# Attention scores accumulated in one bank per head from key differences, with row sums in bursts

## The chip, the cores and the metric

One core of a Trainium2 chip runs the whole kernel. The metric is device time in microseconds, the median over runs; the profile comes from one further execution. The engines are TensorE (PE, with its weight loads PEld), VectorE (DVE), ScalarE (ACT), GpSimd (POOL) and SyncE (SP), whose queue issues most of the DMAs.

## The reference, cut to what matters

A transformer block with conditioning: x is [2, 2048, 512], 16 heads of 32 dimensions, causal attention, then an MLP with hidden width 2048.

```python
mod = silu(condition) @ Wada + bada          # six vectors per batch row
xm  = layernorm(x) * (1 + sc_a) + sh_a
q, k, v = split_heads(xm @ Wqkv)
scores  = where(causal, q @ k.T * hd**-0.5, -inf)
x = x + gt_a * (concat(softmax(scores) @ v) @ Wproj + bproj)
x = x + gt_m * (gelu(modulated_layernorm(x) @ W1 + b1) @ W2 + b2)
```

Everything is float32. The change concerns the scores, the softmax's row sums, and how keys are written and loaded.

## The kernel before, in words

**Stages.** For each of the two batch rows: the QKV products (class `Qkv`), then the attention (`attention_phase`), then the projection. The MLP for both rows comes last. While one row's QKV runs, the first scores of that row are already made.

**QKV.** Four groups (`g`) of 512 tokens. For each group and each chunk `f` of four heads, the q and the k product (four accumulating matmuls each, into a bank named ps_qk) are split into a high and a low part, both in float32r (`hl`, lines 820 to 826: ACT writes the high part, DVE the rest), and written to DRAM by one DMA. Keys and queries are later loaded back so that the 128 partitions hold the 32 dimensions of a head four times, in the combinations high/low of q with high/low of k. One float32r matmul over 128 partitions then gives the score at full precision. `load_keys` does this for keys (`kst`), `load_queries` for queries (`qst`). Two key buffers take turns by chunk.

**Units.** A unit is one chunk of four heads with one block `i` of 512 queries: 16 units per batch row. The softmax needs the row maxima, so each score is computed twice:

- With queries on the partitions (tile `s`, `Row.bank`, `Row.score`): a matmul into a score bank (pool `ps_s`, two banks), then DVE takes the maximum over the keys (`mx`, line 461; with the causal mask on the diagonal block, line 456). These are made up to three units ahead (`AHEAD`). `due` and `count` decide how many are put into each step of the attention, by a cost in about DVE nanoseconds. `Row.rows` turns a unit's maxima into a row vector `fold` (high and low part by head and query tile).
- With keys on the partitions (tile `st`, `scores_t`): for each step, that is each tile `j` of 128 keys, and each of the four heads, a first matmul of 32 partitions (`sel` and `fold`) writes minus the maximum into the head's bank, and a second one adds the score of the keys `kst` with the queries `qst`. ACT then writes the exponential `e` (line 586). On the diagonal, where a key tile meets fewer queries, the tiles that start at query 128 and at 384 share a step and a bank; GpSimd zeroes what lies above the diagonal (line 592).

**After the exponentials.** Two steps later (`LAG`) the values product `o` (`values`, matmuls of 32 columns, one per head, in plain float32) and the row sums `sm` (a product with ones, `row_sums`) follow. For the sums, the exponentials of four full key tiles are first added up (`ee`, line 614, on GpSimd; on DVE in a row's last unit), so that one sums product serves four tiles. `sm` accumulates in a bank of its own through the whole unit; `finish` copies `o` and `sm` out and stores them.

**Order.** Matmuls and most of the work in the attention keep the order in which the program writes them (`keep_in_program_order`, by `mm` and `act`). In a step that is: four folds, then st matmuls and scores alternating, then what `flush` finds due (values and sums), then the remaining scores. Other instructions, those of QKV among them, are ordered by the tile framework. DMAs go into SP's queue in order.

**Banks of PSUM in the attention.** Two for scores, four for st, one for o, one for sm. A score may also borrow an st bank (`borrow`); in the last unit st also uses the score banks.

Of the kernel before, what the change touches and what calls it, by code (L numbers as in the profile page):

```python
# [17 lines left out]
P = 128  # L18
# [9 lines left out]
def dit_block_kernel(  # L28
# [49 lines left out]
    EE_BUFS = 8  # L78
# [5 lines left out]
    def pool(name, bufs=1, **kw):  # L84
# [21 lines left out]
    tmask = bp.tile([P, TQ + 1], F32, tag="tmask", name="tmask")  # L106
    nc.vector.tensor_reduce(
        tmask[:, :TQ],
# [4 lines left out]
    nc.vector.tensor_copy(tmask[:, TQ:], tmask[:, TQ - 1 : TQ])  # L113
    fold, mhl = [], []
    for n in range(2):

        f = bp.tile([P, QB + P], F32R, tag=f"fold{n}", name=f"fold{n}")
        fold.append(f)
# [9 lines left out]
    def picks():  # L128
# [36 lines left out]
        [dram.tile([2, P, T], F32, tag=f"k{b}{c}", name=f"k{b}{c}") for c in range(C)]  # L165
        for b in range(B)
# [38 lines left out]
    def act(ins):  # L205

        return tc.keep_in_program_order(ins)
# [22 lines left out]
    def transposed(pool_, psum, xts, n0, mv, rstd, a, c, b, dst, xns=None):  # L230
# [8 lines left out]
        for t, xt in enumerate(xts):  # L239
            if by_act:  # L240
                continue
            xn = pool_.tile([P, D], F32, tag="xn", name="xn", bufs=3)
            n = n0 + t
            nc.vector.tensor_scalar(
                xn, xt, mv[:, n, 0:1], rstd[:, n : n + 1], ALU.subtract, ALU.mult
            )
            xns.append(xn)
# [41 lines left out]
    class Row:  # L289


        def __init__(self, b):
            self.b = b
            self.vv = bp.tile([P, NT, D], F32, tag="vv", name="vv")
            self.kst, self.qst, self.pools = {}, {}, {0: bp}
# [8 lines left out]
            self.mx = None  # L304
            self.spent = 0
            self.rows_made = 0

        def load_keys(self, c, g, n=1):

            tok = slice(g * MT, (g + n) * MT)  # L310
            if g == 0:
                self.kst[c] = self.pools[c % 2].tile(
                    [P, HC, T], F32R, tag=f"kst{c % 2}", name="kst"
                )
            for r in range(4):
                nc.sync.dma_start(
                    self.kst[c][r * HD : (r + 1) * HD, :, tok].bitcast(F32),
                    kd[self.b][c][r % 2, :, tok].rearrange("(h d) t -> d h t", d=HD),
# [123 lines left out]
        def bank(self, u, h, t, kb, s):  # L442
# [6 lines left out]
                self.kst[c][:, h, kb * QB : kb * QB + w],  # L449
# [41 lines left out]
        def score(self, n, borrow=None):  # L491

            for k in range(n):
                if borrow and k % 2 == 0:
                    s = borrow()
                else:
                    s = ps_sp.tile([P, QB], F32, tag="s", name="s")  # L500
                item = self.todo.pop(0)
                u = item[0]
                if self.mx is None:
                    self.mx = bp.tile(
                        [P, HC * TQ, units[u][1] + 1], F32, tag="mx", name="mx", bufs=3
                    )
                self.bank(*item, s)
                if not self.todo or self.todo[0][0] != u:
# [4 lines left out]
        def rows(self, u):  # L513
# [8 lines left out]
                fold[u % 2].rearrange("p (t q) -> p t q", t=TQ + 1),  # L522
                ps.unsqueeze(1).to_broadcast([P, TQ + 1, P]),
                tmask.unsqueeze(2).to_broadcast([P, TQ + 1, P]),
# [11 lines left out]
    def attention_phase(row):  # L536
        b, vv, kst, qst = row.b, row.vv, row.kst, row.qst
        with pool(f"att{b}") as ap, pool(
            f"ps_st{b}", bufs=HC, space=PSUM
        ) as ps_stp, pool(f"ps_o{b}", space=PSUM) as ps_op:  # L540
            row.pools[1] = ap

            n_bank = [0]

            def scores_t(u, step, n):
# [6 lines left out]

                def st_bank():

                    n_bank[0] += u == len(units) - 1
                    if n_bank[0] % 6 >= HC:
                        return ps_sp.tile([P, QB], F32, tag="s", name="st")
                    return ps_stp.tile([P, QB], F32, tag="st", name="st")  # L560

                c, i = units[u]
                tiles = steps_of[u][step]
                q0 = tiles[0][1]
                w = sum(QB - q for _, q in tiles)
                sts, es = [], []
                for h in range(HC):
                    g = slice(h * HD, (h + 1) * HD)
                    st = st_bank()
                    mm(  # L570
                        st[:, :w], sel[g, :], fold[u % 2][g, q0 : q0 + w],
                        start=True, stop=False,
                    )
                    sts.append(st)
                for h in range(HC):
                    at = 0
                    for j, q in tiles:
                        mm(
                            sts[h][:, at : at + QB - q],
                            kst[c][:, h, j * P : (j + 1) * P],  # L580
                            qst[u][:, h, q:],
                            start=False, stop=at + QB - q == w,
                        )
                        at += QB - q
                    e = ap.tile([P, QB], F32, tag="e", name="e", bufs=E_BUFS)
                    act(nc.scalar.activation(e[:, :w], sts[h][:, :w], AF.Exp))  # L586
                    if tiles[0][0] >= i * TQ:

                        d = e.rearrange("p (t k) -> p t k", k=P)[:, 0 : TQ : TQ - 1, :]
                        d = d[:, : len(tiles), :]  # L590
                        act(
                            nc.gpsimd.affine_select(  # L592
                                d, d, pattern=[[0, len(tiles)], [1, P]],
                                compare_op=ALU.is_ge, fill=0.0,
                                base=0, channel_multiplier=-1,
                            )
                        )
                    es.append(e)
                    if h < 2 and n >= 3 or h >= HC - n and n < 3:
                        row.score(1)  # L600
                if n >= 3:
# [1137 lines left out]
```

## Time and profile before

| | |
|---|---|
| median of 3 runs | 2367.9 us (2367.5 to 2370.27) |
| profiled execution | 2366.88 us, span 2365.2 us |
| granted TensorE clock | 1.00 |
| TensorE busy | 2336.9 us (99%) |
| VectorE, ScalarE, GpSimd busy | 1397.6, 924.1, 1079.2 us |
| fold matmuls (512 and 256 wide) | 1024 and 128 |
| sums matmuls of added tiles | 192, seen as 384 |

The page shows busy time as a union: where matmuls overlap, the time is counted once. A plain float32 matmul is recorded as two matmuls, a float32r matmul as one. In the rows of groups the columns are the line, the engine, the operation, what it writes and reads, the shape and the count, then busy us and mean ns of one, then idle time of the engine before these instructions and what ended it. Line 203 is the helper through which all matmuls go, so groups are told apart by their tiles.

### The profile page before, as it was taken

How to read it: one execution, taken by the hardware profiler on the slowest of the kernel's cores; microseconds unless marked ns; L12 is line 12 of the kernel's file. 1: busy time of each engine (PE TensorE's matmuls, PEld its weight loads, DVE VectorE, ACT ScalarE, POOL GpSimd, SP SyncE). 2: the span in 40 equal slices, each digit the busy share in tenths (PEclk: the TensorE clock that was granted, in tenths of full speed). 3: DMA queues.
4: the chain of work that ended last, by engine and by line, in shares of the span. 5: the costliest groups of instructions: out<-in, count | busy, mean ns of one | idle time of the engine just before them, and what ended most of it. 6: DMA issues, size and time to landing. Idle time of an engine off the chain costs nothing.

```text
span 2365.2 us, 32348 instructions
## 1 busy us (share of the span) xinstructions
PE 2336.9 (99%) x11469; PEld 1294.6 (55%) x11469; DVE 1397.6 (59%) x2868; ACT 924.1 (39%) x1736; POOL 1079.2 (46%) x1219
## 2 busy tenths in 40 slices
PE   8999999999999999999999999999999999999998
PEld 4455555555544445555555555444585486487477
DVE  3466666767656636576666766553483374365356
ACT  2113555555555012155555555613322332332321
POOL 1052997978793646379887997460000000000000
PEclk9999999999999999999999999999999999999999
DMA  7577215151223788650513214272254254353433
GB/s 258 188 249 195 49 28 118 27 117 46 83 106 132 255 259 259 220 113 24 117 46 85 59 31 144 78 252 100 98 170 146 94 179 139 119 166 132 135 124 129
DMA packets 134106, 311.49 MB, mean 132 GB/s; under 512 B 14208, under 2 KB 29100, under 8 KB 129080
## 3 DMA queue, kind: packets, MB, share of 16 engines
q1 hardware_dynamic: 126096, 277.13, 38.9%
q0 software_dynamic: 7472, 31.75, 3.7%
q8 instruction: 90, 1.47, 0.3%
q14 instruction: 72, 0.59, 0.1%
q10 hardware_dynamic: 376, 0.55, 0.1%
HBM read 229.95 MB, written 87.29 MB: 134 GB/s over the span
## 4 chain that ended last, share of the span: by engine, by line
PE 96%; DVE 2%; POOL 1%; issue 0%; DMA 0%; ACT 0%; SPq 0%; POOLq 0%; ACTq 0%; DVEq 0%
PE st L203 20%; PE ps_a L203 17%; PE o L203 11%; PE s L203 10%; PE ps_qk L203 9%; PE ps_b L203 9%; PE ps_v L203 5%; PE ps_o L203 5%; PE ps_c L203 4%; PE sm L203 4%; PE ps_xt L211 1%; POOL ee L614 1%; PE ps_o L211 1%; DVE mx L461 0%; DVE junk L456 0%
## 5 line engine op out<-in xcount | busy, mean ns | idle before, releaser
L586 ACT ACTIVATE e<-st 128x512 f32<-128x512 f32 (+1 forms) x1152 | 574.6, 578 | 428.1 <-PE st L203 361.6
L614 POOL TENSOR_TENSOR ee<-ee,e 128x512 f32<-128x512 f32 x424 | 529.2, 1289 | 4.4 <-ACT e L586 4.0
L461 DVE TENSOR_REDUCE mx<-s 128x1 f32<-128x512 f32 x604 | 407.9, 688 | 204.5 <-PE s L203 203.1
L203 PE MATMUL s<-kst,qst 128*128 128x512 f32 (+3 forms) x1032 | 463.7, 451 | 5.7 <-DVE mx L461 2.9
L203 PE MATMUL st<-qst,kst 128*128 128x512 f32 (+3 forms) x1280 | 409.4, 387 | 0.0
L203 PE MATMUL ps_a<-sum,w 128*128 128x256 f32 (+1 forms) x1088 | 346.6, 454 | 0.0
L203 PE MATMUL o<-e,vv 128*32 128x512 f32 (+3 forms) x2560 | 300.5, 538 | 2.0 <-POOL e L592 2.0
L456 DVE CUSTOM_DVE_ANT_0 junk<-s,causal 128x512 bf16<-128x512 f32 (+3 forms) x428 | 209.3, 489 | 135.5 <-PE s L203 127.6
L203 PEld LDWEIGHTS s<-kst,qst 128*128 128x128 f32 x1032 | 194.4, 189 | 155.7 <-DVE mx L461 55.6
L203 PEld LDWEIGHTS st<-qst,kst 128*128 128x128 f32 x1280 | 227.3, 188 | 94.2 <-issue 62.2
L203 PEld LDWEIGHTS ps_a<-sum,w 128*128 128x128 f32 x1088 | 206.3, 190 | 109.8 <-issue 91.4
L614 POOL TENSOR_TENSOR ee<-e 128x512 f32<-128x512 f32 x168 | 210.4, 1285 | 101.4 <-ACT e L586 101.0
L203 PE MATMUL ps_qk<-xmT,wqkv 128*128 128x512 f32 x512 | 239.0, 594 | 1.8 <-DVE xmT L263 1.8
L592 POOL TENSOR_SCALAR_AFFINE_SELECT e<-e 128x128 f32<-128x128 f32 (+1 forms) x384 | 122.4, 357 | 135.0 <-ACT e L586 132.3
L203 PE MATMUL st<-fold,sel 32*128 32x512 f32 (+1 forms) x1152 | 149.1, 481 | 0.9 <-ACT vv L843 0.5
L203 PEld LDWEIGHTS ps_qk<-xmT,wqkv 128*128 128x128 f32 x512 | 93.9, 190 | 97.0 <-issue 90.4
L1318 DVE TENSOR_TENSOR h<-c,ps_b 128x512 f32<-128x512 f32 x32 | 22.0, 687 | 202.4 <-PE ps_b L203 202.4
L203 PEld LDWEIGHTS st<-fold,sel 32*128 32x128 f32 x1152 | 59.3, 181 | 144.8 <-ACT e L586 86.6
L203 PE MATMUL ps_v<-wqkv,xmT 128*128 128x512 f32 x256 | 122.3, 594 | 0.0
L203 PE MATMUL ps_b<-sum,w 128*128 128x256 f32 (+1 forms) x384 | 120.6, 450 | 0.0
L203 PEld LDWEIGHTS o<-e,vv 128*32 128x32 f32 x2560 | 61.1, 108 | 102.0 <-issue 81.0
L1492 ACT ACTIVATE h<-h,cols 128x512 f32<-128x512 f32 x96 | 69.2, 721 | 118.6 <-DVE h L1318 118.6
(155 smaller groups left out, 2601.3 us busy)
## 6 DMA issues: line engine op xcount, KB each, us to landing
qst<-q SPq DMA_DIRECT2D x128, 256.0 KB
w<-w1d SPq DMA_DIRECT2D x32, 896.0 KB
w<-w2d SPq DMA_DIRECT2D x28, 1024.0 KB
kst<-k SPq DMA_DIRECT2D x24, 1024.0 KB
w<-w2d SPq DMA_DIRECT2D x28, 768.0 KB
q<-hl SPq DMA_DIRECT2D x32, 512.0 KB
k<-hl SPq DMA_DIRECT2D x32, 512.0 KB
w2d<-w POOLq DMA_DIRECT2D x28, 448.0 KB, 6.5
```

The costliest lines, as they stand in the source:

```text
L203: return tc.keep_in_program_order(nc.tensor.matmul(*args, **kw))
L211: return tc.keep_in_program_order(nc.tensor.transpose(dst, src, ident[:n, :n]))
L456: nc.vector.tensor_tensor_reduce(junk[:, :w], s[:, :w], causal[:, QB - w :], 1.0, MASKED, ALU.add, ALU.max, m,)
L461: nc.vector.tensor_reduce(m, s[:, :w], axis=AX.X, op=ALU.max)
L586: act(nc.scalar.activation(e[:, :w], sts[h][:, :w], AF.Exp))
L592: nc.gpsimd.affine_select(d, d, pattern=[[0, len(tiles)], [1, P]], compare_op=ALU.is_ge, fill=0.0, base=0, channel_multiplier=-1,)
L614: act(engine.tensor_tensor(dst, x, y, ALU.add))
L1318: act(nc.vector.tensor_tensor(dst, x, y, ALU.add))
L1492: nc.scalar.activation(d, ps, AF.Gelu, bias=col(r_b1 + half * HF + f, 1))
```

## The change

1. **Key differences.** QKV also writes, for each chunk, `g`: the difference of the keys at token t and at token t - 128, split into high and low parts (`gaps`; `tails` carries the last 128 keys from group to group). It is loaded into one buffer `kgap` for the attention. The old buffer `kst` holds the plain keys, for the scores with queries on the partitions and for unit 0; a new chunk's keys are loaded head by head after the last score of a head (`load_head`), and the differences quarter by quarter (`load_gaps`).
2. **Scores with keys on the partitions.** A unit takes one bank per head for all its steps. The fold matmul runs for the first key tile alone. Every later tile adds the product of the queries with the key difference to what stands in the bank, which turns the scores of tile j - 1 into those of tile j, and ACT reads the exponential from there. Unit 0 works with plain keys and folds in every step. The diagonal tiles are grouped anew: the one from query 128 alone; those from 256 and from 384 in one step, one after the other through the same banks, with the due values in between.
3. **Sums.** Exponentials are added in pairs, not fours. The sums products are collected and come in bursts into a bank that is held only for a burst; its result is copied out by ACT (the unit's first) or added by DVE (`partial`).
4. **Third score bank.** Outside a burst, that bank serves as a third one for scores, in turn with the other two (`free_bank`); no st bank is borrowed any more, and st doesn't use score banks.
5. **Around it.** The normalization writes over its input (`xn = xt`), the high and low parts are separate half buffers with a DMA each (six), and 12 `ee` buffers take the place of 8.

```diff
-    EE_BUFS = 8
+    EE_BUFS = 12
...
-            xn = pool_.tile([P, D], F32, tag="xn", name="xn", bufs=3)
+            xn = xt
...
+        def load_head(self, c, h):
+            for r in range(4):
+                nc.sync.dma_start(
+                    self.kst[r * HD : (r + 1) * HD, h, :].bitcast(F32),
+                    kd[self.b][c][r % 2, h * HD : (h + 1) * HD, :],
+                )
+        def load_gaps(self, c, g):
+            tok = slice(g * MT, (g + 1) * MT)
+            for r in range(4):
+                nc.sync.dma_start(
+                    self.kgap[r * HD : (r + 1) * HD, :, tok].bitcast(F32),
+                    gd[self.b][c][r % 2, :, tok].rearrange("(h d) t -> d h t", d=HD),
+                )
...
+        def free_bank(self):
+            self.turn = (self.turn + 1) % 3
+            if self.third and self.turn == 0:
+                return self.third()
+            return ps_sp.tile([P, QB], F32, tag="s", name="s")
...
+                if i == NQ - 1 and c + 1 < C and self.todo[0][:2] != (u, h):
+                    self.load_head(c + 1, h)
...
+                keys = row.kgap if u else kst
+                at = 0
+                for k, (j, q) in enumerate(tiles):
+                    if k:
+                        values()
+                    if j == 0 or u == 0:
+                        for h in range(HC):
+                            g = slice(h * HD, (h + 1) * HD)
+                            mm(
+                                sts[h][:, q:], sel[g, :], fold[u % 2][g, q:],
+                                start=True, stop=False,
+                            )
+                    for h in range(HC):
                         mm(
-                            sts[h][:, at : at + QB - q],
-                            kst[c][:, h, j * P : (j + 1) * P],
+                            sts[h][:, q:],
+                            keys[:, h, j * P : (j + 1) * P],
                             qst[u][:, h, q:],
-                            start=False, stop=at + QB - q == w,
+                            start=False, stop=True,
+                            skip_group_check=u > 0 and j > 0,
                         )
...
+            def partial(held, sm):
+                if held:
+                    act(nc.vector.tensor_tensor(held[0], sm, held[0], ALU.add))
+                    return
+                held.append(ap.tile([P, QB], F32, tag="sums", name="sums"))
+                act(nc.scalar.copy(held[0], sm))
...
-                + [[(i * TQ + 1, P), (i * TQ + 3, 3 * P)], [(i * TQ + 2, 2 * P)]]
+                + [[(i * TQ + 1, P)], [(i * TQ + 2, 2 * P), (i * TQ + 3, 3 * P)]]
...
+                    if u % NQ == NQ - 1 and c + 1 < C and n_step in (5, 9, 13):
+                        row.load_gaps(c + 1, n_step // TQ - 1)
+                    elif u % NQ == 0 and c and n_step == 1:
+                        row.load_gaps(c, NG - 1)
...
+                        if n_step % 2 == 0:
                             even = es
-                        elif k == 1:
+                        else:
                             chain = begin_chain(u, even, es)
-                        else:
-                            add_to(u, chain, es)
-                        if k == TQ - 1 and n_step + 1 < i * TQ:
-                            sums_of, wait = (chain, False), 2
+                            parts.append((chain, ((0, 0),)))
+                        if n_step % TQ == TQ - 1 and n_step + 1 < i * TQ:
+                            burst = LAG + 1
...
+        def gaps(self, g, f, ps, hp, tok):
+            kf = hp.tile([P, P + MT], F32, tag="kf", name="kf", bufs=2)
+            tail = self.tails[:, f, :]
+            if g == 0:
+                nc.vector.memset(kf[:, :P], 0.0)
+            else:
+                nc.scalar.copy(kf[:, :P], tail)
+            nc.scalar.copy(kf[:, P:], ps)
+            if g + 1 < NG:
+                nc.scalar.copy(tail, kf[:, MT:])
+            d = kf[:, :MT]
+            nc.vector.tensor_tensor(d, kf[:, P:], d, ALU.subtract)
+            self.split(d, 1.0, hp, gd[self.row.b][f], tok)
+
+        def split(self, src, scale, hp, dst, tok):
+            def half():
+                return hp.tile([P, MT], F32R, tag="hl", name="hl", bufs=self.halves)
+            hi, lo = half(), half()
+            nc.scalar.activation(hi, src, AF.Copy, scale=scale)
+            nc.sync.dma_start(dst[0, :, tok], hi.bitcast(F32))
+            nc.vector.scalar_tensor_tensor(
+                lo, src, scale, hi.bitcast(F32), ALU.mult, ALU.subtract
+            )
+            nc.sync.dma_start(dst[1, :, tok], lo.bitcast(F32))
```

## The prediction, made before the changed kernel was run

> **What bounds the kernel now.** I read the page first: busy time by engine, and the chain that ended last.
>
> ```profile
> PE 2336.9 (99%) x11469; PEld 1294.6 (55%) x11469; DVE 1397.6 (59%) x2868; ACT 924.1 (39%) x1736; POOL 1079.2 (46%) x1219
> PE 96%; DVE 2%; POOL 1%; issue 0%; DMA 0%; ACT 0%; SPq 0%; POOLq 0%; ACTq 0%; DVEq 0%
> ```
>
> TensorE carries 96% of the chain, so a microsecond less of matmuls in its queue is a microsecond less of time, until another engine makes it wait. Then I cut the first row of the batch (the second is its twin) into stretches: QKV, attention with scoring of later units, attention after the last score (columns: busy us of PE, PEld, DVE, ACT, POOL, then clock, DMA share, GB/s):
>
> ```profile
> 60.00:212.50 152.50, 152.45 (x461) 75.92 (x459) 87.74 (x217) 27.50 (x49) 37.81 (x54) 1.00 0.66 214
> 212.50:693.60 481.10, 478.59 (x3244) 251.41 (x3244) 327.42 (x804) 265.77 (x530) 406.26 (x455) 1.00 0.32 78
> 693.60:752.00 58.40, 56.76 (x385) 23.97 (x387) 36.94 (x60) 38.42 (x78) 25.20 (x33) 1.00 0.22 74
> ```
>
> In the scoring stretch DVE works 68% of the time, ACT 55%, POOL 84%. The groups by form name the fold matmuls, the row sums of added tiles, and the maxima that empty the score banks:
>
> ```profile
> L203 PE MATMUL st<-fold,sel 32*128 32x512 f32 x1024 | 135.9, 493 | 0.8 <-ACT vv L843 0.5
> L203 PE MATMUL sm<-ee,ones 128*32 128x512 f32 x384 | 52.3, 604 | 0.0
> L461 DVE TENSOR_REDUCE mx<-s 128x1 f32<-128x512 f32 x604 | 407.9, 688 | 204.5 <-PE s L203 203.1
> ```
>
> Because matmuls overlap, prices are read from start to start in the timeline of TensorE (start us, duration):
>
> ```profile
> 459.31 1.06 PE L203 MATMUL sm<-ee,ones 128*32 128x512 f32 x8
> 460.19 1.04 PE L203 MATMUL o<-e,vv 128*32 128x512 f32 x8
> 461.16 0.50 PE L203 MATMUL s<-kst,qst 128*128 128x512 f32 x1
> 461.59 0.50 PE L203 MATMUL st<-fold,sel 32*128 32x512 f32 x4
> 462.03 0.50 PE L203 MATMUL st<-qst,kst 128*128 128x512 f32 x1
> 462.36 0.40 PE L203 MATMUL s<-kst,qst 128*128 128x512 f32 x1
> 462.60 0.39 PE L203 MATMUL st<-qst,kst 128*128 128x512 f32 x1
> ...
> 463.98 1.07 PE L203 MATMUL o<-e,vv 128*32 128x512 f32 x8
> 464.97 0.51 PE L203 MATMUL st<-fold,sel 32*128 32x512 f32 x4
> 465.41 0.50 PE L203 MATMUL st<-qst,kst 128*128 128x512 f32 x1
> ```
>
> To see: a fold group of four costs 0.44 us until the first st; a score (s) ahead of a fold takes 0.43 instead of the 0.24 that it takes ahead of an st; a sums group takes 0.88; the values (o) take 0.99 whatever follows.
>
> **The change part by part** (both batch rows together; counts from the order of instructions of the two kernels).
>
> Fold matmuls. 512-wide groups fall from 256 to 32: 224 x 0.44 = 98.6 us. 256-wide groups fall from 32 to 2: 30 x 0.32 = 9.6 (426.55 to 426.87 in the same timeline). Four narrower groups come in u = 0: 1.2 back. In about 96 of the 256 places a score or st stands ahead of the fold and pays 0.2 us for the change of shape; nine tenths of these go: 17. Together 124 us off TensorE's queue, all on the path.
>
> The same rows against a rule: the Trainium skill's page "TensorE: Matmul & The Clock Gate" (section "Measured speedup vs the span model") gives four K=32 matmuls in different row groups the span of one matmul plus some 4 ns for each further one, and the section "Back-to-back issue gap" gives 0.216 us for one of 512. An estimate by that page would be 254 x 0.23 = 58 us saved instead of 124, and a forecast of about 2407 us, slower than before. The trace shows 0.44 and is used.
>
> Sums. Pairs instead of fours make 384 sums matmuls out of 192, which is 48 more groups of four: 48 x 0.88 = 42 us added. They stand in bursts beside o, so no other change of shape is added. POOL loses 168 adds of 1.29 us (592 to 424): 216 us off an engine that is off the path; worth nothing (ACT waits for POOL's ee 10 us in all, which is the most it could give).
>
> So TensorE's queue gets 82 us shorter. What is late next:
>
> (a) Diagonal tiles. The last two tiles now go one after the other through the same four banks, and directly after the last one (four 128-wide st) stands the next unit's fold, which writes these banks. Four exponentials must end first. ACT takes 0.52 us for each of four 512-wide ones and 0.37 for a 256-wide one (the timeline shows 2.07 for four and 0.74 for two); a 128-wide one isn't shown, about 0.3 by the same slope. From the first 128-wide st: some 0.3 until ACT starts, 1.2 for four; TensorE has 0.4 of st and mostly one score (0.3 to 0.4) to do meanwhile. It idles about 0.8 us at 30 unit changes: 24 us. Ends: 0.4 (two scores between, cheaper exponentials) and 1.3 (no score, 0.37 each), 12 to 39. This wait doesn't exist before, where o (0.99) stood between. ACT's extra exponentials (128 of 128 wide, some 20 us) lie inside its idle 45%.
>
> (b) Score banks. Two score banks, and the third where it isn't lent to the sums. DVE empties a 512-wide bank in 0.61 to 0.69. The shorter step (some 3.1 us with four scores) still holds 4 x 0.65 = 2.6 of DVE, so with three banks I count nothing. The third bank is away for 1 step at 12 mid-unit bursts and 1 or 2 steps at 16 unit ends of a row, 36 scoring steps of 129: there every third score 0.47 us apart waits for a reduction that ends 0.1 to 0.4 later, 0.3 (four scores) to 0.6 (five) a step, say 0.35 x 72 = 25 us. Before, similar waits cost about 8 us a row (the rows name only single ones, such as 0.18 and 0.64 us at 215.8 and 219.9), so +9, and 7 for the 24 added DVE sums and masked scores: 16. Ends: -10 (three banks remove the old waits too) and 50 (0.2 us in every scoring step).
>
> (c) The sums take over the third bank. At 24 mid-unit bursts the sums stand directly behind the last st and wait if one of the last scores sits in that bank: 0.95 if the last one, 0.3 if the one before, else 0; mean 0.4: 10 us. Ends 0 and 23. At unit ends an o stands between: nothing.
>
> (d) Key differences in QKV. Each of 16 k products a row adds on ACT a 512-wide copy (0.59), a split (0.60 from PSUM, 0.81 from SBUF in the row of L1230) and two 128-wide copies (under 0.38 each); on DVE a subtraction and a second split (0.73 and 0.69): some 32 and 23 us a row where they idle 125 and 65 of 152.5. What hides them is TensorE, busy 152.45. In order, however, a difference on DVE that waits for ACT holds back the maxima behind it, and with scores 1.09 us apart in two banks TensorE stops once DVE is more than 1.1 us late. 24 of the 32 lie where scores run: ends 0 and 1.5 us each (the two operations in a row); I take 0.25, since 1.42 us of work only just passes the slack: 6 us, at most 36. SP issues 145 more DMAs at 0.36 to 0.5 us, off the path: 8.4 MB of differences are written per row within 152 us, 55 GB/s on top of 214 (row 0) and 248 (row 1), where the page's best slice shows 259. A late write keeps one of six half buffers; a pair of products takes 7.5 to 10 us, several landings long.
>
> (e) Loads. The difference keys of chunk 0 start where the second key buffer's load started (212.61 us), 1 MB first, needed at u = 1 some 8 us later; later quarters are asked for a unit ahead. Key loads by head leave 12 short scores (some 7 us of DVE) for the last 1 MB. SP waits there for a score, and behind it stand only stores of o and sums and query loads that nobody needs within microseconds. Nothing; 1 us at 6 heads if short.
>
> In-place normalization costs nothing: the x loads wait for transposes long done. Projection and MLP (from 1543 us) are untouched.
>
> Sum: -82 + 24 + 16 + 10 + 6 = -26 us. The profiled execution took 2366.9 (span 2365.2, 1.7 around it), 1.0 under the median of 2367.9. 2366.9 - 26 = 2341.
>
> **Rivals.** *The waits stay small* (half of a, none of b to d): -82 + 12 = 2297. For it: in the stretch TensorE's named waits are under 3 us in all today. Against: a is in the order of the instructions.
>
> *DVE becomes the bound of the scoring steps*, and it ends slower. It has 327 us of work in 481; with TensorE's share down by some 35 us a row it stands at 73%, but a step of five 512-wide scores asks 3.25 of a step of 3.3, and the split score banks give no room to even out. At 0.5 us in each of 258 scoring steps: +129, 2470 at worst; it decides from (82 - 24 - 10 - 6) / 258 = 0.16 us a step. As a usual size take 0.28: 2395. The Trainium skill's page "TensorEngine Tiling" (section "PSUM Bottleneck") warns that a faster TensorE can leave the emptying of PSUM as the limit; no row here shows DVE saturated.
>
> *QKV stalls* by the differences: at 1.5 us in 24 places and 16 us more for late DMA writes, 2341 + 46 = 2387, slower.
>
> *The fold was covered anyway* (TensorE waited for ACT under it): then the 124 shrinks. The last unit, without scores, has steps of 2.55 us against ACT's 2.07, so at most 0.05 of the 0.44 there could stay: 28 x 0.05, negligible.
>
> **How the numbers follow.** Forecast 2341 (2315 to 2362): 0.45. Small waits, 2297: 0.22. Within 0.2% (5 us, about what a measurement of this kernel can tell): 0.08. DVE bound: 0.17. QKV stalls: 0.08. So faster 0.67, same 0.08, slower 0.25. The range leaves out the lowest and the highest tenth: 2288 (small waits, and nothing at all for b to d) to 2398 (the usual size of the DVE case).
>
> **What would show it.** Fold groups: 38 of four, near 20 us. Scoring stretch 481 to about 465, attention without scores 58 to 53; 512-wide st starting right after o. TensorE idle before fold, released by ACT's e, 20 to 30 us (a); idle before s, released by DVE mx (b); before sm, by DVE mx (c). QKV within 3 us of 152.5. I'm wrong if TensorE's queue isn't 70 to 90 us shorter by counts times starts, or if s waits for mx by more than 40 us.

## The result, and the profile after

The changed kernel takes 2438.4 us (median of 4 runs, 2434.5 to 2441.7), the kernel before 2367.7 (2367.1 to 2370.3) on the same chip: 1.030 times as long, 95% interval 1.028 to 1.031. The forecast was 2341. The profiled execution took 2441.7 us (span 2439.9), 74.8 more than that of before.

The page of the changed kernel, busy time by engine and the chain that ended last:

```profile
PE 2334.9 (96%) x10853; PEld 1255.9 (51%) x10853; DVE 1429.6 (59%) x2939; ACT 1005.0 (41%) x1976; POOL 877.0 (36%) x1051
PE 38%; DVE 1%; POOL 0%; issue 0%; ACT 0%; DVEq 0%; ACTq 0%
```

TensorE's busy time is the same as before to 2 us, with 616 fewer records in it, and its share of a longer span fell from 99% to 96%. A busy microsecond is not always a useful one: a record of a 512-wide st is 0.39 to 0.40 us long, while the next matmul can start 0.23 us after it (timeline below), so the first 0.17 us of a wait count as busy. DVE is at 59% as before.

Now by stage. I cut both traces at the first matmul of QKV, the last of its values, the last score and the last values of the attention (the rows below begin at 60 us, as in the prediction, so the first is a part of its stage). Columns as there: busy us of PE, PEld, DVE, ACT, POOL, then clock, DMA share, GB/s.

```profile
60.00:229.30 169.30, 158.47 (x462) 77.61 (x460) 106.13 (x245) 50.76 (x101) 38.47 (x54) 0.98 0.75 241
229.30:730.20 500.90, 475.35 (x2982) 233.29 (x2981) 327.12 (x817) 282.34 (x589) 307.20 (x374) 0.99 0.43 102
730.20:787.00 56.80, 55.78 (x381) 24.26 (x377) 29.00 (x47) 39.52 (x85) 25.80 (x37) 0.97 0.46 163
```

QKV from 60 us on is 169.3 us long instead of 152.5, the scoring stretch 500.9 instead of 481.1, the rest of the attention 56.8 instead of 61.4 (the prediction's row of 58.4 ends at 752, some 3 us before this stage does). POOL lost 99 us of work in the scoring stretch, which bought nothing. Whole stages of all kernels, in us, from such cuts (QKV of rows 0 and 1; scoring stretches of both; the 61 us of attention behind them and the rest moved by less than 8 us a row):

| kernel | QKV 0 | scoring 0 | QKV 1 | scoring 1 | time |
|---|---|---|---|---|---|
| before | 194.0 | 481.6 | 190.7 | 481.5 | 2367.7 |
| changed | 211.1 | 501.4 | 216.9 | 503.3 | 2438.4 |
| differences in QKV alone (e1) | 213.7 | 480.7 | 220.9 | 486.4 | 2419.0 |
| attention alone (e2) | 194.6 | 502.0 | 189.1 | 501.5 | 2396.4 |
| without their stores (e6) | 199.7 | 500.6 | 195.0 | 500.3 | 2404.3 |
| two score banks (e3) | 214.9 | 535.4 | 211.4 | 537.7 | 2505.7 |
| half maxima (e5) | 211.2 | 475.5 | 215.6 | 476.1 | 2388.6 |
| scores spread (e12) | 210.7 | 483.5 | 215.6 | 486.9 | 2407.0 |

So the loss has two halves of different origin: QKV +17.1 and +26.2, 43 us together; attention +15 and +16 (scoring +20 and +22, less 5 and 6 behind it).

What TensorE waits for: the weight load of a score stands ahead of it and waits for the bank (waiting line, releaser, us in total, times, longest). In the changed kernel:

```profile
PEld s L206 <- DVE mx L480: 166.8, 311, 3.5
PEld s L206 <- DVE mx L475: 77.7, 134, 4.7
PE s L206 <- DVE mx L480: 17.6, 32, 3.1
PE s L206 <- DVE mx L475: 16.2, 19, 3.9
PE s L206 <- DVE fold L546: 12.4, 26, 1.0
```

and in the kernel before, for its first batch row alone:

```profile
PEld s L203 <- DVE mx L461: 25.8, 36, 0.8
PEld s L203 <- DVE mx L456: 15.3, 22, 0.8
```

In the same row's attention (229.3 to 787 us) the changed kernel has 72.2 us in 138 and 27.1 in 57. A load's wait is partly covered by the matmul that still runs. What is lost is seen from start to start, in the timeline of TensorE behind a unit change, and of DVE at the same time:

```profile
321.17 0.42 PE L206 MATMUL s<-kst,qst 128*128 128x384 f32 x1
322.62 0.50 PE L206 MATMUL s<-kst,qst 128*128 128x512 f32 x1 [1.03 <-DVE fold L546]
322.96 0.39 PE L206 MATMUL st<-qst,kgap 128*128 128x512 f32 x1
323.19 0.40 PE L206 MATMUL s<-kst,qst 128*128 128x512 f32 x1
323.43 0.40 PE L206 MATMUL st<-qst,kgap 128*128 128x512 f32 x1
323.90 0.50 PE L206 MATMUL s<-kst,qst 128*128 128x512 f32 x1
324.24 0.39 PE L206 MATMUL st<-qst,kgap 128*128 128x512 f32 x1
```

```profile
321.27 0.69 DVE L661 TENSOR_TENSOR sums<-sm,sums 128x512 f32<-128x512 f32 x1 [2.44 <-issue]
321.88 0.68 DVE L546 TENSOR_TENSOR fold<-ps_m,tmask 128x512 fp32r<-128x512 f32 x1
322.48 0.55 DVE L475 CUSTOM_DVE_ANT_0 junk<-s,causal 128x384 bf16<-128x384 f32 x1
323.16 1.29 DVE L480 TENSOR_REDUCE mx<-s 128x1 f32<-128x512 f32 x2
```

To see: st to score takes 0.23 us where the bank is free (322.96 to 323.19) and 0.47 where it isn't (323.43 to 323.90); no idle time is named there, because the record of the st before it lasts until 323.83. The bank comes free with a maximum: the first of the two in the row at 323.16 takes some 0.65 us. And the score behind a wait needs 0.34 to the next st (323.90 to 324.24), 0.10 more than the one at 323.19.

For the account below I took every start-to-start distance of neighbouring matmuls in the attention of both rows and called *excess* what lies over the tenth percentile of the same pair of shapes in the compared kernels. Before: 1083 us, 978 of base and 105 of excess. Changed: 1116, 912 and 204. The excess at pairs with a score (st then score, score then st, score then score) rose from 30 + 7 + 7 to 76 + 46 + 16, that is 44 to 138. How pairs are grouped matters to some 10 us: other groupings give 83 to 90 for this rise of 94.

### The profile page after: what moved, and what is told of

Same layout as the page of the kernel before. It is cut to its first block, busy times and chain, and to the rows that moved or that the text cites. A ratio compares the mean times of both kernels' runs of the same rounds, so it can differ in the third digit from the quotient of the medians.

```text
span 2439.9 us, 31311 instructions
## 1 busy us (share of the span) xinstructions
PE 2334.9 (96%) x10853; PEld 1255.9 (51%) x10853; DVE 1429.6 (59%) x2939; ACT 1005.0 (41%) x1976; POOL 877.0 (36%) x1051
## 5 line engine op out<-in xcount | busy, mean ns | idle before, releaser
L611 ACT ACTIVATE e<-st 128x512 f32<-128x512 f32 (+3 forms) x1280 | 607.1, 538 | 413.3 <-PE st L206 353.1
L206 PE MATMUL s<-kst,qst 128*128 128x512 f32 (+3 forms) x1280 | 571.5, 459 | 59.7 <-DVE mx L480 17.6
L480 DVE TENSOR_REDUCE mx<-s 128x1 f32<-128x512 f32 x768 | 506.4, 686 | 192.9 <-PE s L206 190.1
L639 POOL TENSOR_TENSOR ee<-e 128x512 f32<-128x512 f32 x336 | 421.0, 1286 | 295.6 <-ACT e L611 291.7
L206 PE MATMUL st<-qst,kgap 128*128 128x512 f32 (+3 forms) x1248 | 432.8, 379 | 0.0
L475 DVE CUSTOM_DVE_ANT_0 junk<-s,causal 128x128 bf16<-128x128 f32 (+3 forms) x512 | 248.4, 485 | 126.8 <-PE s L206 116.7
L206 PEld LDWEIGHTS st<-qst,kgap 128*128 128x128 f32 x1248 | 226.6, 190 | 79.4 <-ACT e L611 46.3
L206 PE MATMUL ps_qk<-xmT,wqkv 128*128 128x512 f32 x512 | 244.5, 605 | 1.8 <-DVE xmT L266 1.8
L206 PE MATMUL sm<-ee,ones 128*32 128x512 f32 x768 | 103.7, 618 | 11.4 <-DVE mx L475 4.7
L639 POOL TENSOR_TENSOR ee<-ee,e 128x512 f32<-128x512 f32 x88 | 110.3, 1291 | 0.0
L206 PEld LDWEIGHTS ps_b<-sum,w 128*128 128x128 f32 x384 | 73.0, 190 | 37.2 <-issue 30.6
```

What stands on the lines that cost most here:

```text
L206: return tc.keep_in_program_order(nc.tensor.matmul(*args, **kw))
L475: nc.vector.tensor_tensor_reduce(junk[:, :w], s[:, :w], causal[:, QB - w :], 1.0, MASKED, ALU.add, ALU.max, m,)
L480: nc.vector.tensor_reduce(m, s[:, :w], axis=AX.X, op=ALU.max)
L611: nc.scalar.activation(es[h][:, at : at + QB - q], sts[h][:, q:], AF.Exp)
L639: act(engine.tensor_tensor(dst, x, y, ALU.add))
```

## The experiments

All ratios are against the kernel before, in runs on the same chip.

**Which half is it? (e1, e2)** Into the kernel before, the differences alone, made, split and stored as in the changed kernel and loaded by nobody, with 6 and 5 half buffers:

```
+                    self.split(ps, HD**-0.5 if which == 0 else 1.0, hp, dst, tok)
+                    if which == 1:
+                        self.gaps(g, f, ps, hp, tok)
```

> The kernel before, with the key differences made in QKV, split and stored (and the half buffers, six in row 0 and five in row 1, and the normalization in place), but never loaded: attention is as before. Theory A (two separate losses: QKV waits because ACT waits for half buffers and differences, DVE waits for ACT in order, and the scores wait for DVE; attention loses by score banks): about +43 us, 2411 (2400 to 2420), the QKV stretches 17 and 26 us longer. Rival B (QKV only looks longer because the changed attention's loads and pools press on it): 2375 or less.

Measured 2419.0 us, 1.022 [1.020, 1.023]: +51, QKV +19.7 and +30.2 of it, as theory A has it. Then the changed kernel without them:

```
-                    if which == 1:
-                        self.gaps(g, f, ps, hp, tok)
-                    gd[self.b][c][r % 2, :, tok]...
+                    kd[self.b][c][r % 2, :, tok]...
```

> The changed kernel without making or storing differences: the difference buffer is loaded from the plain keys instead, and the exponential's input is scaled by 0.001, so attention does the same work on other numbers. Theory A: QKV back to its time before, attention as in the changed kernel: 2438 - 43 = 2395 (2385 to 2405), still slower than before by 27. Rival B: QKV stays long, 2430 or more.

Measured 2396.4, 1.012 [1.011, 1.014]: QKV is back at 194.6 and 189.1, attention stays as slow as in the changed kernel. The two losses are separate: the differences alone cost 51, the new attention alone 28, and the sum of 79 is near the 71 measured (e1 has one half buffer less in row 1, which e11 below prices at 5).

**What makes QKV late? (e6, e8, e11, e17)** First everything computed, but the differences not stored:

```
-            self.split(d, 1.0, hp, gd[self.row.b][f], tok)
+            self.split(d, 1.0, hp, None, tok)
```

> The changed kernel, with the key differences copied, subtracted and split in QKV as there, but not stored; attention loads plain keys in their place (exponentials scaled by 0.001 so that they stay finite), so that the output is not the reference's. Theory D1: QKV is late by the transfers (stores ahead of the x loads on SP, half buffers kept by stores): both QKV stretches fall by 25 us or more of the 43 that they grew, 2395 to 2413 us. Theory D2: QKV is late by the operations on ACT and DVE, which hold the maxima behind them: both stretches keep 30 or more of the 43, 2425 to 2440 us.

Measured 2404.3, 1.016 [1.014, 1.017], QKV -11.4 and -21.9: 33 of the 43 us hang on the stores, 10 on the added operations of ACT and DVE. How TensorE comes to stop is seen in the changed kernel at 896 to 914 us, DVE first and then TensorE:

```profile
898.44 0.08 DVE L475 DVE_READ_ACCUMULATOR2_ANT mx<- 128x1 f32 x1
907.66 0.69 DVE L218 BATCH_NORM_STATS2 stat<-x 128x6 f32<-128x512 f32 x1 [9.14 <-DMA x<-in_x_dram]
908.86 0.55 DVE L475 CUSTOM_DVE_ANT_0 junk<-s,causal 128x384 bf16<-128x384 f32 x1
909.34 0.68 DVE L887 SCALAR_TENSOR_TENSOR hl<-ps_qk,hl 128x512 fp32r<-128x512 f32 x1
...
910.51 1.39 DVE L218 BATCH_NORM_STATS2 stat<-x 128x6 f32<-128x512 f32 x2 [0.40 <-DMA x<-in_x_dram]
...
912.62 0.67 DVE L475 CUSTOM_DVE_ANT_0 junk<-s,causal 128x512 bf16<-128x512 f32 x1
```

```profile
909.47 0.33 PE L206 MATMUL s<-kst,qst 128*128 128x128 f32 x1 [3.92 <-DVE mx L475]
913.36 0.58 PE L206 MATMUL s<-kst,qst 128*128 128x256 f32 x1 [2.54 <-DVE mx L475]
```

DVE stands 9.14 us at the statistics of an x tile whose load lands late, and no maximum is taken meanwhile: that of 908.86 stands behind them in DVE's order. TensorE stops twice for want of a score bank, the first time with DVE idle, the second time while DVE works off the statistics that were held up (910.51 to 912.62). A half buffer whose store hasn't landed does the same at 177 us:

```profile
173.53 0.68 DVE L887 SCALAR_TENSOR_TENSOR hl<-ps_qk,hl 128x512 fp32r<-128x512 f32 x1
177.17 0.69 DVE L887 SCALAR_TENSOR_TENSOR hl<-ps_qk,hl 128x512 fp32r<-128x512 f32 x1 [2.95 <-DMA k<-hl]
177.78 0.41 DVE L475 CUSTOM_DVE_ANT_0 junk<-s,causal 128x256 bf16<-128x256 f32 x1
```

```profile
178.25 0.50 PE L206 MATMUL s<-kst,qst 128*128 128x512 f32 x1 [3.36 <-DVE mx L475]
```

Then the same stores from POOL's queue:

```
-            self.split(d, 1.0, hp, gd[self.row.b][f], tok)
+            self.split(d, 1.0, hp, gd[self.row.b][f], tok, nc.gpsimd)
```

> The changed kernel, with the stores of the key differences issued from POOL's queue, not SP's; the bytes stay. Under D1 with SP's queue as the cause (x loads stand behind stores that wait for their operand): 2410 to 2425 us, the later row gaining most. Under D1 with the bytes as the cause, or under D2: 2432 to 2445.

Measured 2480.6, 1.048 [1.046, 1.050]: a miss for both readings, and the clearest hint. QKV 1 grew to 249.1 us. POOL has weights of the MLP in hand there (14.7 us in one piece from 958.26 on, the next store of differences at 976.54) and issues the stores late; the halves stay taken (ACT's and DVE's waits, e8, 880 to 1110 us):

```profile
ACT hl L885 <- DMA g<-hl: 55.1, 7, 14.8
```

```profile
DVE hl L887 <- DMA g<-hl: 29.1, 4, 10.0
```

Not all of the 42 us on top of the changed kernel are these waits themselves: TensorE's clock stood at half for 65 us of the two QKV stages, against 17 in the changed kernel (see the last section).

So the number of half buffers, 9 in row 0 and 5 in row 1 instead of 6 and 6 (the kernel before has 4 and 3 pairs, 8 and 6 halves, for two thirds of the stores):

```
-            qkv.run(hp, also, 6)      # row 0
+            qkv.run(hp, also, 9)
-            qkv.run(hp, also, 6)      # row 1
+            qkv.run(hp, also, 5)
```

> The changed kernel with 9 buffers for the halves of queries, keys and differences in batch row 0 and 5 in batch row 1, where it has 6 in both. Theory H (QKV is late because halves stay taken until their stores land): the QKV stretch of row 0 falls from 211 us to 198 to 206, that of row 1 grows from 217 to 222 or more. Rival X (the stores' bytes delay the x loads and key loads, buffers don't matter): both stretches within 3 us of 211 and 217, total within 6 of 2438.

Measured 2431.4, 1.027 [1.025, 1.028]: QKV 0 fell to 205.7, QKV 1 rose to 222.3, both inside theory H. And the x loads out of SP's queue:

```
-                nc.sync.dma_start(xt, x_rows(...))
+                act(nc.scalar.dma_start(xt, x_rows(...)))
```

> The changed kernel with the x loads issued from ACT's queue, not behind the stores of halves in SP's queue. If the order in SP's queue is what makes the normalization on DVE wait (15.3 us in 9 waits for x in the changed kernel), these waits go and QKV gets 8 to 15 us shorter: 2423 to 2430 us. If the halves or the bytes are the cause: within 5 of 2438, and ACT's splits are held where an x load waits for its buffer (worse than 2443 if much).

Measured 2434.3, 1.028 [1.026, 1.029]: the total lies in the second range, but QKV 0 fell to 199.8 while QKV 1 stayed (216.1); the first matmul of QKV 0 starts 6.6 us later, since the first x loads now stand in ACT's queue. So in row 0 both the halves (-5.4) and the place of the x loads behind the stores count (-11.3, as far as the later start of the stage does not help it). In row 1, where DMA works at 0.81 and 261 GB/s over the stage, only the buffers and the stores themselves were shown to matter.

**What makes the scores wait? (e3, e5, e4)** The third bank never used for scores:

```
-            if self.third and self.turn == 0:
+            if False and self.turn == 0:
```

> The changed kernel with the third bank never used for scores (two banks always, the sums keep theirs). Theory A: the steps outside bursts, 0.06 us of wait per score after an st, become like those inside (0.16): some 50 us more, 2490 (2465 to 2510). Rival C (DVE's rate sets the pace, not the number of banks): 2430 to 2450.

Measured 2505.7, 1.058 [1.056, 1.060], as theory A has it; excess 272 instead of 204. Then the plain maxima over half of their columns, so that DVE's work shrinks and TensorE's doesn't:

```
-                nc.vector.tensor_reduce(m, s[:, :w], axis=AX.X, op=ALU.max)
+                nc.vector.tensor_reduce(m, s[:, : w // 2], axis=AX.X, op=ALU.max)
```

> The changed kernel with each unmasked maximum taken over half of its keys only (other numbers result): 768 reductions of about 0.4 us in place of 0.69, some 220 us of DVE work away. Theory A: scores wait little for banks, attention 35 to 45 us shorter per row: 2355 to 2375. Rival D (scores wait because DVE itself waits in order, for sums and ACT, not for its own work): at most 25 us less, 2413 or more.

Measured 2388.6, 1.008 [1.006, 1.010]: 50 us less, less than the 63 to 83 expected, but well off the rival. Emptying the banks is a cause; 46 us of excess stay above before (151 against 105). Then DVE's adds of the sums, at which DVE stands 60.8 us (the edit also leaves 11 of the 12 `ee` buffers, not shown here):

```
-                    act(nc.vector.tensor_tensor(held[0], sm, held[0], ALU.add))
+                    t = ap.tile([P, QB], F32, tag="more", name="more")
+                    act(nc.scalar.copy(t, sm))
+                    act(nc.gpsimd.tensor_tensor(held[0], t, held[0], ALU.add))
```

> The changed kernel, but the sums of a later burst are copied out of their bank by ACT and added by POOL, not by DVE. In the changed kernel's trace DVE stands in order at those adds: 60.8 us in 18 waits for the sums matmuls, with the maxima of later scores queued behind. Theory A: this wait holds the score banks; TensorE gets back about 1 us at each of 24 bursts inside a unit and some at 30 unit ends: 2405 to 2425 us. Rival: DVE had the time to spare, and scores wait because one maximum takes 0.65 us whatever stands around it: 2433 or more.

Measured 2434.4, 1.028 [1.026, 1.030]: the theory fell. The wait seen at 321 us is real, but without 18 such waits the attention is only 6 us shorter (1115.6 to 1109.4).

**Number or place? (e9, e12, e18)** Sums from fours again (one line that concerns a row's last unit isn't shown here):

```
-                        if n_step % 2 == 0:
+                        if n_step % TQ == 0:
                             even = es
-                        else:
+                        elif n_step % TQ == 1:
                             chain = begin_chain(u, even, es)
                             parts.append((chain, ((0, 0),)))
+                        else:
+                            add_to(u, chain, es)
```

> The changed kernel, with sums from fours of key tiles again (one group of four matmuls in a burst inside a unit in place of two), the rest as changed. Plain count: 48 groups of 0.88 us, 42 us less on TensorE. Theory A: the third bank is also lent for less time and DVE waits less for the sums, so 42 to 55 us come back: 2383 to 2396 us. Rival: DVE sets the pace of the scoring steps, and what TensorE saves comes back as waits: 2415 or more. Third case: POOL, with its 168 adds of 1.29 us back, is late with the added tiles and TensorE waits for them: between the two, with waits of sums for POOL in the trace.

Measured 2416.0, 1.020 [1.017, 1.024]. The groups of sums take 93.8 us instead of 143.3, yet the attention is only 22 us shorter: half comes back as waits. The total stands at the border between the rival (2415 or more) and the third case. What the trace has of the third case is not the wait of sums that it named, but one of the values for POOL's masks (e9):

```profile
PE o L206 <- POOL e L620: 14.6, 19, 1.4
```

Then only the place of the scores within the step:

```
-                        if not k and (h < 3 and n >= 3 or h >= HC - n and n < 3):
+                        if not k and (h != 1 and n >= 3 or h >= HC - n and n < 3):
```

> The changed kernel with the first three scores of a step after the first, third and fourth st, not after the first, second and third; their number stays. Theory S (scores wait because they follow each other in 0.47 us where DVE empties a bank in 0.65): waits of scores fall and the scoring stretches get 8 to 15 us shorter each: 2408 to 2423 us. Rival N (the number of maxima against the length of a step decides, wherever the scores stand): within 6 of 2438, or longer, because the third score moves closer to the last ones of the step.

Measured 2407.0, 1.016 [1.015, 1.018], 31 us less, by the place of two scores in a step, and 1 us more of a gain than theory S had at most. The same scoring stretch of row 0 is 483.5 us long, with the same records on TensorE and DVE:

```profile
229.50:713.00 483.50, 461.43 (x2983) 237.13 (x2981) 329.99 (x818) 271.76 (x589) 306.73 (x374) 1.00 0.45 106
```

DVE's work is unchanged (330 us, 327 before the edit), so the total of its work was not the limit. Three scores 0.47 us apart meet a reduction of 0.65 to 0.69: with each of them DVE falls some 0.2 us behind, and a score waits where no bank is empty by then, in a stretch in a third of which DVE idles. Some of the gain is clock, though: the profiled attention of the changed kernel has 24 us at half clock, that of e12 3 us, which is up to 10 of the 35 us by which it got shorter (1115.6 to 1080.1). By the mean clocks of all runs (0.991 to 0.993 against 0.993 to 0.994) it is some 5 of the 31, an estimate. The other place, behind the values:

```
-                        if not k and (h < 3 and n >= 3 or h >= HC - n and n < 3):
+                        if not k and (h in (0, 2) and n >= 3 or h >= HC - n and n < 3):
-                return es, max(0, n - 3)
+                return es, n - 2 if n >= 3 else 0
```

> The changed kernel with two scores of a step after the first and third st and the others (one to three) after the values. Spread alone (three scores after the first, third and fourth st) measured 2407. If the place of a score decides through its distance to the next ones, scores in a row behind the values, 0.24 us apart, wait for the banks that the step's first ones left: 2412 to 2430 us. If only the distance inside the st counts: within 6 of 2407.

Measured 2428.8, 1.025 [1.023, 1.026], within the first reading: compared with e12, excess behind an st is the same, and that of a score behind a score is 20 to 45 us more, by how the pairs are grouped. Where they wait moves with where they are crowded.

**The bursts, and the kernel before (e19, e22)** Spread scores, and no bursts of sums inside a unit:

```
                         if n_step % TQ == TQ - 1 and n_step + 1 < i * TQ:
-                            burst = LAG + 1
+                            parts = []
```

> The kernel with spread scores (2407), with the bursts of sums inside a unit left out: the sums of those tiles are missing from the result, their additions on POOL stay. The third bank is lent only at unit ends. Plain: 24 bursts of 1.71 us and 14 us of waits of sums for maxima go: 2345 to 2355 us. If the lent bank costs the scores of the steps around a burst as well: 2325 to 2342 us.

Measured 2346.9, 0.991 [0.989, 0.993], 60 less than with spread scores and 5 more than the plain sum of 55 (24 bursts of 1.71 us and 14 of waits). The bank that is lent inside a unit costs the scores around it hardly anything once they are spread (excess behind an st 52 to 48 us). Lending at unit ends was not taken away. And the kernel before with its second score moved behind the third st:

```
-                    if h < 2 and n >= 3 or h >= HC - n and n < 3:
+                    if h in (0, 2) and n >= 3 or h >= HC - n and n < 3:
```

> The kernel before with one edit: its second score of a step stands after the third st and not after the second. Its scores lose some 30 us behind an st in the trace. If the distance between scores is what these waits come from: 2352 to 2364 us, faster than before. If not, because the change of shape ahead of the fold or the borrowed bank decides there: 2365 to 2375.

Measured 2368.8, 1.000 [0.999, 1.001]: a miss for the first reading. Its excess behind an st is 28 us as against 30, so in this kernel it is not the distance of the two scores that these waits come from. Whether it is the fold and change of shape in each step or the borrowed bank that decides, no run shows.

**Together (e16, e20)** Both kernels combine edits shown above. Fours, spread scores and 9 halves in row 0; then also the x loads from ACT's queue:

> Sums from fours, scores after the first, third and fourth st, and 9 buffers for halves in row 0, together. By the sum of their single effects: fours alone measured -22; with S another -16 to -30, with H another -5 to -13: 2373 to 2395 us. With neither: 2410 to 2420.

> Sums from fours, spread scores, 9 half buffers in row 0, x loads from ACT's queue: all single effects that helped. Fours, spread and 9 buffers measured 2392.5; the x loads alone gave 11 us in the QKV stretch of row 0, of which the 9 buffers have taken half: 2380 to 2390 us. It stays behind the kernel before by what the stores of row 1 cost.

Measured 2392.5, 1.010 [1.008, 1.012] and 2398.7, 1.012 [1.010, 1.015]. The first is within what was expected, at its upper end: fours bring little once the scores are spread (1080.9 us of attention, 1080.1 without them; TensorE waits 22.2 us for POOL's masks). The second is a miss: QKV 0 fell to 195.3, but its first matmul starts 6.0 us later and attention and QKV 1 took 1.8 and 2.9 more. No arrangement tried that keeps the whole computation reaches the kernel before: with attention brought back to its 1083 us, the stores of the differences remain.

## Why the prediction was wrong

By its own terms, against the traces:

| term | forecast | measured |
|---|---|---|
| TensorE's queue: fold, sums, changes of shape | -82 | -66 |
| (a) fold waits for exponentials | +24 | +3 |
| (b) score banks | +16 (-10 to 50) | +94 |
| (c) sums wait for the third bank | +10 (0 to 23) | +13 |
| other pairs in the attention | 0 | -11 |
| (d) differences in QKV | +6 (0 to 36) | +43 |
| sum | -26 | +76 (74.8 in the profiled executions) |

*The queue.* The mechanism was right: 38 groups of fold are left, as forecast, 28.3 us start to start instead of 129.8, some 12 of it now waiting; without waits that is -105 for -107 forecast. Sums grew by 47 for 42 forecast. The changes of shape gave 8 of the 17 hoped for. Trusting the row of 0.44 us was right: the estimate of 58 us saved, which followed from the Trainium skill's page "TensorE: Matmul & The Clock Gate", section "Measured speedup vs the span model", does not fit the 105 measured. The 66 in all lie just outside the 70 to 90 that the prediction named as its sign.

*(a)* was oversized: the fold waits 12 us in all, the low end, and similar waits of 9 existed before.

*(b) is the step that failed most.* "The shorter step (some 3.1 us with four scores) still holds 4 x 0.65 = 2.6 of DVE, so with three banks I count nothing" compares a sum over a step with the length of the step. A bank doesn't wait for the sum; it waits for the reduction that stands before it, and three scores stood 0.47 us apart. I had used this distance for two banks in 36 steps only. Over 258 scoring steps 94 us are 0.36 a step. The sign named for it, more than 40 us of s waiting for mx, is 33.8 as idle time of TensorE and was too narrow: the weight loads ahead of the scores stand for 244.5, where they stood for 89.3 before. The rival "DVE becomes the bound of the scoring steps" had 0.16 as the point from which it decides and 0.28 as its usual size: the price was near, the reason not. DVE is busy 327 of 501 us, no more than before, and e12 gives back 35 us of attention at the same work. So it is not the total of DVE's work, against which the rival was weighed, but place and number of banks: e12 accounts for 35 of the 94 (up to 10 of them clock), e3 shows what one bank fewer costs. (The rival's own sum counts (b) twice: its worst case comes to 2454, not 2470, and its usual size to 2397, which stands there as 2395 and 2398.) What the other 59 or so are made of in shares (unit ends with the bank lent, masked maxima, the 0.1 us behind each wait, the clock) stays open; e5 shows that quicker emptying takes 50 us off, e4 and e19 that the sums' adds and the bursts inside a unit are not it.

*(d) failed too*, by its bound: 43 against at most 36. I counted the added operations of ACT and DVE, of which e6 leaves 10 us, and costed the stores at nothing ("a pair of products takes 7.5 to 10 us, several landings long", "one of six half buffers"). The number of stores rose by half while row 0 lost two buffers, and e11 and e17 show both the buffers and the queue behind them. The rival "QKV stalls by the differences" had the size (46), with another inside. It was given 0.08 and priced as if alone.

*The range* was made of cases one at a time, so that its upper end, 2398, was one rival's price. Both came true together, and nothing excluded that: e1 and e2 show that they are independent.

*In-place normalization costs nothing*, *(e) loads* and the hidden fold needed no correction: e2 keeps the normalization in place and has QKV at 194.6 and 189.1 us as before, and no load of keys or differences appears among TensorE's longest waits.

## What to carry to other kernels

Before shortening the busiest engine's queue, look at what the removed work kept apart: lay the remaining consumers of each scarce buffer out on a time line and compare the distance between two of them with the time in which that buffer is emptied, not the sums over a step. Then move one of them to see whether the distance counts: here it did in the changed kernel (e12) and not in the kernel before (e22). Count added stores as occupants of the buffers that they read, and look which in-order engine stands behind the next free one. Two rivals that act in different stages can both come true, and then their prices add.

## What was not expected of the hardware

TensorE's granted clock, 1.00 in the stages shown of before, falls to half for 3.4 or 6.8 us behind some of the gaps, short ones too. The page's groups don't show it; windows do. Around a burst of sums that waited for a maximum ((c) of the prediction), TensorE's timeline of the changed kernel, and windows from there and from behind the two stops at 909 and 913 us shown above (columns as in the table of stages, the clock third from the end):

```profile
290.70 0.40 PE L206 MATMUL st<-qst,kgap 128*128 128x512 f32 x1
292.58 3.62 PE L206 MATMUL sm<-ee,ones 128*32 128x512 f32 x16 [1.48 <-DVE mx L475]
```

```profile
286.00:290.00 4.00, 3.32 (x18) 1.39 (x17) 2.92 (x12) 2.26 (x5) 3.77 (x4) 1.00 1.01 238
292.50:295.90 3.40, 3.32 (x16) 1.00 (x20) 0.00 (x0) 0.00 (x0) 0.00 (x0) 0.52 0.02 5
296.50:300.00 3.50, 3.50 (x23) 1.46 (x17) 2.07 (x9) 2.54 (x5) 1.57 (x2) 1.00 0.00 0
913.30:916.80 3.50, 3.44 (x6) 1.68 (x6) 3.46 (x11) 1.81 (x4) 2.38 (x4) 0.50 0.86 196
```

The burst of eight matmuls, 1.71 us elsewhere, takes 3.33 (to the o at 295.91). The trace has nine such stretches, 41 us together, so up to 20 us are lost on top of the gaps themselves. 24 of the 41 us lie in the attention, so up to 12 us of what the table above books as excess are clock, and 17 in QKV, up to 9 of its 43. In the profiled attention of e3 and e5 there are none, in that of e4 3 us, so e4's 6 us may be clock alone. The Trainium skill's page "TensorE: Matmul & The Clock Gate", section "HAM oscillation — how this bites in real kernels", gives as the rule that there be no idle gaps over some 3.4 us. Here such a stretch began right behind a gap of 1.48 us in which nothing ran, and another at one of 1.49 that ended at 1125.8; two longer ones, of 3.36 us up to 178.3 and 3.06 up to 956.1, had no such stretch directly behind them, so length alone does not decide, and what does stays open.

Also: behind a wait for a bank the matmul that waited took 0.10 us more to the next one (0.34 at 323.90, 0.24 at 323.19), so a wait costs more than its length.
